# Layer 0 of a four-layer graph network: one excursion per tile, projections between weighing groups, the node bias hoisted, and the last norm in two parts

## The chip, the cores and the metric

The kernel runs on one core of a Trainium2 chip. The metric is the device time of one execution in microseconds. A core has five engines with queues of their own: TensorE (PE, with its weight loads counted apart as PEld), VectorE (DVE), ScalarE (ACT), GpSimd (POOL) and SyncE (SP, which here only issues transfers). Each engine takes its instructions in order. An instruction that waits holds up everything behind it on its engine, and nothing on the others, until one of them needs a result.

The kernel before takes 1303.24 us (median of 3 executions, 1303.01 to 1305.43).

## The reference

Four graph layers, each followed by a residual sum and a layer norm over the last axis. N is 2048 nodes, the batch B is 8, and there are C = 64 features. Only layer 0 and the first operations of layer 1 matter here.

```python
# layer 0, K = 3 polynomials of the adjacency matrix A, D = 16
w = einsum('nd,dkio->nkio', embedding, weight)      # weights per node
b = einsum('nd,do->no', embedding, bias)            # bias per node
As = [I, A, 2 A A - I]
x_g = einsum('knm,bmc->bnkc', stack(As), x)
out = einsum('bnki,nkio->bno', x_g, w) + b
x = layernorm(x + out)
# layer 1 begins with
h = x @ W
s = leaky_relu(h @ a_node, 0.2)                     # score of a node
alpha = softmax over nodes of s where H.T > 0
agg = einsum('ben,bnf->bef', alpha, h)
beta = sigmoid((h @ a_gn)[:, None, :] + (agg @ a_ge)[:, :, None])
industry = einsum('nm,bmf->bnf', adj / deg, x @ W_ind)
```

The later layers multiply by the adjacency matrix again and project; the change does not touch them.

## The kernel before

**Stages of layer 0.** Nodes go in 16 tiles of 128 (P = 128, NT = 16). The values of a tile, 8 batch elements of 64 features, are 512 columns (BC), and batch elements go in four pairs (NP), so that one transposed pair fills 128 partitions. `first_product` computes y1 = A x in 32 pieces of 16 matmuls, in four quarters of four tiles each, into accumulators of seven PSUM banks (`acc0`). The mask of non-zeros of A is multiplied, with x split in a high and a low part, and the row's scale is applied when the sum is read out (`y_hi` on ACT, `y_lo` on DVE). The weights `w0`, the embedding and the bias are loaded by `load_w0` (L235).

`layer0` (L1039) then goes through the tiles. For one tile j it holds:

- `weigh(j, g)`, L1172, for g = 0 to 7. Group g is half of the batch (4 elements) times 4 of the 16 embedding components. It makes 12 matmuls of 64 rows and 256 columns (the terms x, A x and A A x, for two pairs and two halves of the partitions), each recorded as two, into one of the two tiles of the pool `pps0` (two banks each), and then four `scalar_tensor_tensor` operations on DVE (L1193), which multiply by an embedding component and add into the residual `r`. The order in which they add is a chain on one buffer.
- `product(j)`, L1140: 32 matmuls of 512 columns that give A (A x) for the tile; ACT copies the result to `y` (L1151). `first_terms(j)`: transposes of A x and the node bias, one matmul of the transposed embedding `et` with `bias_sb` (L1126), and POOL's sum r0 = x + bias (L1131). `second_term(j)`: transposes of A A x.
- `scaled`, `compare`, `mask` and `degrees(j)`, L1080 to 1167: DVE makes the mask of the next tiles (L441), POOL scales it and sums it, DVE compares it with the matrix, and PE sums it to the degrees that later layers use. POOL's sum of both halves is called `both`.
- `normed(j, step)`, L1197: layer norm in three steps on DVE and ACT.
- For layer 1: `to_features(j)` (transposes of the normed x), `project(j)` (L1262 on, 16 matmul records, W and W_ind side by side in `wb`, into a `pps0` tile, read out by ACT and DVE), `scores(j)` (L1249, matmuls of 4 columns with `wa`), the weights exp(s), POOL's weighted features and their low part, and `gather(j)` (L1318), which adds to agg in a PSUM bank of its own.

**PSUM in layer 0.** The eight banks: one for layer 1's early product `fi`, one for agg (`fag`), two for transposes and small results (`trs0`, tag "tr"), and four for `pps0`.

**What sets the order.** `program_order()` (L212) fixes the written order on PE, DVE, ACT and POOL. The order of SP's transfers is left to the scheduler. The loop in L1389 to 1454 writes, after each group g of tile j, work for other tiles. Four times per tile there is work of 128 rows between groups of 64 rows: after g2 `first_terms(j+1)`, after g3 the projection, `product(j+1)` and `to_features(j-1)`, after g6 `second_term(j+1)`, `scores(j-1)` and `gather(j-2)`, after g7 `degrees(j+1)`:

```python
elif g == 3:
    when(j - 2, project)
    ...
        for _ in product(j + 1):
    ...
    when(j - 1, to_features)
...
elif g == 6:
    when(j + 1, second_term)
    when(j - 1, scores)
```

A last turn j = NT has no weighing; it is called the tail here. It holds the norm, transposes, scores and projection of tile 15, the denominators of the softmax (`denominators`, 32 small matmuls) and `industry_early`, the first of layer 1's products for the industry term: 16 steps of two matmuls of 512 columns, eight of them in the tail (five and three), seven in the beginning of layer 1 (four, one, two, at L598 to 620), and the last in the written sequence of layer 1's ramp, `early[0](NT)` at L1005. Buffers of layer 0 have homes in 16 slots of the retired split of x (`homes`, L1048).

## Time and profile before

| What | Value |
|---|---|
| Median of 3 executions | 1303.24 us |
| Profiled execution, its own time | 1302.44 us |
| Span of the profiled execution | 1300.7 us |
| Mean granted clock of TensorE | 0.976 |
| First product and its preparation | 0 to about 137 us |
| First weighing group of tile 0, of tile 1, of tile 2, of tile 15 | 156.71, 196.01, 228.03, 664.35 us |
| End of weighing | 691.14 us |
| DVE's first read of agg in layer 1 (L584) | 708.57 us |
| Three stretches of the span: PE busy | 126.80 of 131.00, 560.99 of 580.00 (131 to 711), 558.57 of 589.70 |

The profile is one execution, traced. The span goes from its first to its last instruction; the time has 1.74 us more around it. Busy times add up what an engine's instructions took. Matmuls are pipelined, and the ends of the records are modelled, so that prices of PE work are best read as differences between starts. "Waited for" names the engine whose result came last by the record. A page line gives busy us, share of the span and the number of instructions.

### The profile page before, as it was taken

What the parts mean: (1) busy time and instruction counts of PE and PEld (TensorE: products, weight loads), DVE (VectorE), ACT (ScalarE), POOL (GpSimd) and SP (SyncE); (2) the same over time, 40 slices, a digit from 0 to 9 for tenths busy, and PEclk for the clock granted to TensorE, in tenths of its full rate; (3) what the DMA queues carried; (4) which work ended last, traced back from release to release, by engine and by line L of the source; (5) the groups of instructions that cost most, each with busy time, mean ns of one, the idle gap of its engine ahead of it and who ended that gap; (6) DMA issues with size and microseconds to landing.
All of it is one profiled execution on the core that took longest, in us unless ns stands there. A gap on an engine that the chain in (4) does not pass through costs nothing. (4 is left out here: it accounts for less than half of the span.)

```text
span 1300.7 us, 20049 instructions
## 1 busy us (share of the span) xinstructions
PE 1246.4 (96%) x7724; PEld 1002.3 (77%) x7724; DVE 891.8 (69%) x1601; ACT 378.0 (29%) x853; POOL 512.1 (39%) x418
## 2 busy tenths in 40 slices
PE   9999789999999999999998799999998899999996
PEld 8787568888888888888886477777766788888885
DVE  4555268888887877888665777777774656565544
ACT  3000101221222222222222356666665521111111
POOL 1000354555554555555521578888871600000000
PEclk9999889999999999999999699999998999999998
DMA  8889533323333323222262322232220223334541
GB/s 283 249 236 174 179 97 102 107 99 106 108 108 108 108 100 97 95 97 105 81 234 66 113 76 98 102 102 99 84 83 1 97 98 130 121 106 154 194 170 67
DMA packets 100951, 157.22 MB, mean 121 GB/s; under 512 B 12912, under 2 KB 64496, under 8 KB 94832
## 3 DMA queue, kind: packets, MB, share of 16 engines
q1 hardware_dynamic: 98368, 151.65, 36.0%
q10 hardware_dynamic: 2304, 4.20, 0.8%
q8 instruction: 63, 1.03, 0.3%
q0 software_dynamic: 176, 0.02, 0.1%
q14 instruction: 40, 0.33, 0.1%
HBM read 118.08 MB, written 37.76 MB: 120 GB/s over the span
## 5 line engine op out<-in xcount | busy, mean ns | idle before, releaser
L1193 DVE SCALAR_TENSOR_TENSOR r<-pp,emb_sb,r 128x256 f32<-128x256 f32 x512 | 247.3, 483 | 110.2 <-PE pp L1182 95.4
L1182 PE MATMUL pp<-w_sb,xT 64*128 64x256 f32 x1024 | 161.5, 392 | 6.5 <-DVE r L1193 6.5
L1182 PE MATMUL pp<-w_sb,y2T 64*128 64x256 f32 x1024 | 154.6, 378 | 0.0
L1182 PE MATMUL pp<-w_sb,y1T 64*128 64x256 f32 x1024 | 154.6, 378 | 0.0
L1131 POOL TENSOR_TENSOR r<-xs,bn 128x256 f32<-128x256 f32 x32 | 22.7, 731 | 245.8 <-issue 217.2
L1182 PEld LDWEIGHTS pp<-w_sb,xT 64*128 64x128 f32 x1024 | 95.0, 187 | 24.7 <-issue 9.7
L1182 PEld LDWEIGHTS pp<-w_sb,y1T 64*128 64x128 f32 x1024 | 100.5, 188 | 11.0
L1182 PEld LDWEIGHTS pp<-w_sb,y2T 64*128 64x128 f32 x1024 | 100.4, 188 | 11.1
L524 PE MATMUL y1p<-x_hi,m 128*128 128x512 f32 x256 | 102.9, 402 | 1.0 <-DVE y_lo L539 1.0
L1145 PE MATMUL y2p<-y_hi,msk 128*128 128x512 f32 x256 | 103.5, 404 | 0.0
L1520 PE MATMUL ind<-y_hi,mj_l 128*128 128x512 f32 x240 | 101.8, 424 | 0.2 <-DVE dlt L843 0.2
L1145 PE MATMUL y2p<-y_lo,msk 128*128 128x512 f32 x256 | 101.4, 396 | 0.0
L524 PE MATMUL y1p<-x_lo,m 128*128 128x512 f32 x256 | 100.8, 394 | 0.2 <-DVE x_lo L464 0.2
L1520 PE MATMUL a<-v_hi,mj_l 128*128 128x512 f32 x256 | 100.1, 392 | 0.0
L1520 PE MATMUL a<-v_lo,mj_l 128*128 128x512 f32 x256 | 100.0, 391 | 0.0
L1520 PE MATMUL a<-y_lo,mj_l 128*128 128x512 f32 x240 | 95.1, 396 | 0.0
L1520 PE MATMUL a<-y_hi,mj_l 128*128 128x512 f32 x240 | 94.9, 395 | 0.0
L1520 PE MATMUL ind<-y_lo,mj_l 128*128 128x512 f32 x240 | 94.5, 394 | 0.0
L1084 POOL TENSOR_TENSOR ms<-msk,srow 128x1024 f32<-128x1024 f32 x32 | 90.2, 2819 | 10.0 <-DVE msk L441 5.1
L794 POOL TENSOR_TENSOR ez<-ez,coef 128x1024 f32<-128x1024 f32 x32 | 69.9, 2184 | 48.5 <-DVE ez L789 48.5
L441 DVE TENSOR_SCALAR msk<-adj 128x1024 fp32r<-128x1024 f32 x32 | 61.9, 1971 | 1.2 <-DMA adj<-in_at 1.2
L1145 PEld LDWEIGHTS y2p<-y_hi,msk 128*128 128x128 f32 x256 | 48.9, 191 | 13.0 <-issue 1.0
(294 smaller groups left out, 2434.1 us busy)
## 6 DMA issues: line engine op xcount, KB each, us to landing
mj_l<-mask SPq DMA_DIRECT2D x46, 1024.0 KB, 4.9
adj<-in_at SPq DMA_DIRECT2D x64, 256.0 KB, 3.9
mask<-msk SPq DMA_DIRECT2D x32, 512.0 KB, 4.6
raw<-in_at SPq DMA_DIRECT2D x31, 512.0 KB, 5.5
oh<-oh SPq DMA_DIRECT2D x32, 128.0 KB, 4.2
xT<-in_xt SPq DMA_DIRECT2D x16, 256.0 KB, 2.9
xs<-in_xn SPq DMA_DIRECT2D x16, 256.0 KB, 2.9
kept<-x SPq DMA_DIRECT2D x16, 256.0 KB, 2.0
```

What stands on the lines that cost most here:

```text
L441: nc.vector.tensor_scalar(r_(m), raw, 0.0, None, op0=ALU.is_gt)
L524: nc.tensor.matmul(accs[q][jj], r_(m[:, t, jj * P:(jj + 1) * P]), r_(part[:, mt, :]), start=i + h + t == 0 and part is x_hi, stop=i == 3 a ...
L794: nc.gpsimd.tensor_tensor(by_b(ezs[i]), by_b(ezs[i]), per_b(t["coef"], 2 * i, 2), ALU.mult)
L1084: nc.gpsimd.tensor_tensor(ms, m, srow[j].unsqueeze(1).to_broadcast([P, 8, P]), ALU.mult)
L1131: nc.gpsimd.tensor_tensor(r[:, 4 * bq * C:4 * (bq + 1) * C] .rearrange("p (h l c) -> p h l c", h=2, l=2), swapped(terms[j]["xs"], bq), bn. ...
L1145: nc.tensor.matmul(acc, r_(msk[j, mt // 8][:, mt % 8, :]), r_(part[:, mt, :]), start=mt == 0 and part is y_hi, stop=mt == NT - 1 and part ...
L1182: nc.tensor.matmul(pp[:, h, pl, :], terms[j][name][rs, 2 * bq + pl], w_sb[rs, k, dq * 4 * C:(dq + 1) * 4 * C], start=k == 0, stop=k == K - 1,)
L1193: nc.vector.scalar_tensor_tensor(rb, ppv[:, :, dd, :], emb_sb[:, j, d:d + 1], rb, op0=ALU.mult, op1=ALU.add)
L1520: nc.tensor.matmul(acc, r_(a[:, mt, :]), r_(part[:, mt, :]), start=mt == 0 and part is hi, stop=mt == NT - 1 and part is lo,)
```

## The change

**Node bias.** The bias of all 16 tiles is computed in the first product, at its second piece, into two of the accumulators, read out by ACT one piece later, and kept in `bn_all`. The transposed embedding comes by four transfers on ACT's queue into slots of `y_lo` that are not yet in use. The loads of `et` per tile, the bias matmul and its copy leave the loop.

**Weights.** `w0` and the embedding are fetched in seven pieces during pieces 10 to 16 of the first product, instead of by three transfers that are written after it.

**Excursion.** All work of 128 rows for a tile stands in one place, `visit(j)` after group 4. POOL's sum of the parts of A x (`first_sum`) is a function of its own, after g1, and r0 (`begin_sum`) is written after g5 of the tile before. `x` of a tile (`xs`) has one buffer instead of two, and is loaded after the tile before has read it.

**Projections.** `project` comes in two halves, after g5 and g7 (each with six copies on ACT and two subtractions on DVE), into the banks of the transposes. Two score columns stand beside W and W_ind in `wb` (130 columns), so that the scores come out of the projection; `scores` and `wa` are gone. The vectors for these columns are made after g5 of tile 0 (`score_weights`), not after its first group.

**Last tile.** Its norm, transposes, projections, weights and gathers come in halves of the batch (`half_normed`, `last_tile`), the first half's norm during g5 to g7. The tail holds two steps of `industry_early`; layer 1's ramp, which takes what is left, holds seven.

**Small.** Layer 1's constants `minus1` and `mhalf` are set on POOL instead of DVE. Buffers move between homes; the squares of the norm share the home of `y2`.

```diff
 def first_product(...):
+            def node_bias():
+                et, bn_all, rest = bias_in
+                b0 = bn_all[0:D, NT - 1, :]
+                for half in range(2):
+                    bp = ps_acc.tile([P, NT // 2, C], F32, tag="acc", name=f"bp_{half}")
+                    for t in range(NT // 2):
+                        j = half * (NT // 2) + t
+                        nc.tensor.matmul(
+                            bp[:, t, :], et[j // 4][0:D, (j % 4) * P:(j % 4 + 1) * P], b0,
+                            start=True, stop=True,
+                        )
...
+                    if n == 1:
+                        node_bias()
+                    elif n == 2:
+                        keep_bias()
+                    elif 10 <= n < 11 + 2 * K:
+                        midway(n - 10)
...
-        nc.vector.memset(minus1, -1.0)
+        nc.gpsimd.memset(minus1, -1.0)
...
-        def first_terms(j):
-            tr = ps_tr.tile([P, NP, P], F32, tag="tr", name=f"try1_{j}")
+        def first_sum(j):
             if j > 1:
-                y1 = tile("y1", f"y1_{j}", bufs=1)
-                nc.gpsimd.tensor_tensor(y1, y_hi[:, j, :], y_lo[:, j, :], ALU.add)
...
-            bp = ps_tr.tile([P, QW], F32, tag="tr", name=f"bp_{j}")
-            nc.tensor.matmul(bp[:, 0:C], terms[j]["et"], bias_sb, start=True, stop=True)
-            bn = tile("bn", f"bn_{j}", (P, C))
-            nc.scalar.copy(bn, bp[:, 0:C])
...
+        def half_normed(bq, step):
+            j = NT - 1
+            cols, bs = slice(4 * bq * C, 4 * (bq + 1) * C), slice(4 * bq, 4 * bq + 4)
...
+            elif step == 1:
+                nc.vector.tensor_reduce(var[:, bs], b_view(sq)[:, bs, :], AX.X, ALU.add)
+                nc.vector.tensor_scalar(var[:, bs], var[:, bs], EPS, None, op0=ALU.add)
+                nc.gpsimd.tensor_tensor(rstd[:, bs], var[:, bs], mhalf[:, bs], ALU.pow)
...
-        def scores(j):
...
+        def projected(j, n):
+            mms[j, n] = [
+                ps_tr.tile([P, 2, 2 * C + 2], F32, tag="tr", name=f"hp_{j}_{n}_{h}")
+                for h in range(2)
+            ]
+            for r in range(2):
                 for h in range(2):
...
+        def project(j, n):
+            projected(j, n)
+            for what in ("hi", "h", "sc", "lo"):
+                copied(j, n, what)
...
+        def weighted(j):
...
+            nc.gpsimd.tensor_tensor(r_(lo), hs, hi, ALU.subtract)
...
+        def visit(j):
+            when(j - 2, gather)
+            if j < NT - 1:
+                when(j - 1, normed, 2)
+            when(j + 1, compare, 0)
+            when(j + 1, first_terms)
+            if j + 1 < NT:
+                for _ in product(j + 1):
+                    pass
+            when(j + 2, mask, 0)
+            when(j + 2, mask, 1)
+            when(j + 1, compare, 1)
+            when(j - 1, to_features)
...
+            when(j + 1, second_term)
+            when(j + 1, degrees)
+
+        def last_tile():
+            trail = ("hi", "lo")
+            early.extend(industry_early())
+            half_features(0)
+            gather(NT - 2)
+            projected(NT - 1, 0)
+            half_normed(1, 0)
...
+            denominators(0, NT - 1)
+            half_normed(1, 1)
+            weights_of(NT - 1, slice(0, 4))
+            half_weighted(0)
+            half_gather(0)
...
+            half_normed(1, 2)
+            half_features(1)
+            projected(NT - 1, 1)
+            copied(NT - 1, 1, "sc")
+            weights_of(NT - 1, slice(4, 8))
+            half_weighted(1)
+            early[0](2)
+            denominators(NT - 1, NT)
+            half_gather(1)
...
                 for g in range(8):
-                    when(j, weigh, g)
+                    weigh(j, g)
...
                     elif g == 1:
+                        if j == 0:
+                            degrees(0)
+                        when(j + 1, scaled, 1)
+                        when(j + 1, first_sum)
+                    elif g == 2:
                         when(j - 1, normed, 1)
...
+                    elif g == 4:
+                        visit(j)
...
                     elif g == 5:
+                        if j == 0:
+                            score_weights()
+                        when(j + 2, scaled, 0)
+                        when(j + 1, begin_sum)
+                        when(j + 2, load_xs)
+                        when(j - 1, project, 0)
+                        if j == NT - 1:
+                            half_normed(0, 0)
+                            project(j - 1, 1)
+                            weights_of(j - 1)
...
+                    elif g == 7 and j < NT - 1:
+                        when(j - 1, project, 1)
+                        when(j - 1, weights_of)
+                        when(j - 1, weighted)
                     elif g == 7:
-                        when(j + 1, degrees)
-            early[0](3)
-            gather(NT - 1)
+                        half_normed(0, 2)
+            last_tile()
+            early.pop(0)
```

## The prediction

> **What bounds the kernel now.** I read the page first, for the engines:
>
> ```profile
> PE 1246.4 (96%) x7724; PEld 1002.3 (77%) x7724; DVE 891.8 (69%) x1601; ACT 378.0 (29%) x853; POOL 512.1 (39%) x418
> ```
>
> TensorE (PE) leads, but the change touches layer 0 alone, so I cut that layer into its stages with the view that gives busy time by stretch (start:end, length, then busy us of PE, its weight loads, DVE, ACT, POOL, and the granted clock):
>
> ```profile
> 131.00:156.70 25.70, 16.49 (x67) 12.73 (x65) 5.02 (x9) 3.92 (x7) 10.25 (x9) 0.80 0.64 211
> 156.70:196.00 39.30, 34.61 (x241) 27.99 (x240) 25.39 (x49) 1.55 (x4) 19.86 (x20) 0.91 0.29 89
> 228.00:664.30 436.30, 436.14 (x3448) 367.95 (x3448) 349.37 (x642) 98.03 (x196) 225.02 (x191) 1.00 0.33 111
> 664.30:691.10 26.80, 24.98 (x223) 22.13 (x223) 19.64 (x49) 6.60 (x13) 4.55 (x6) 1.00 0.30 82
> 691.10:708.60 17.50, 14.77 (x101) 12.21 (x100) 6.96 (x17) 4.35 (x10) 5.03 (x4) 0.90 0.10 31
> ```
>
> Tiles 2 to 14 (third row) leave PE 0.16 us idle in 436: there only fewer or shorter PE instructions help, and PE must stay fed. The handover from the first product, tile 0, tile 15 and the tail have holes. The waits of PE between 131 and 711 us name them (total, times, longest):
>
> ```profile
> PE pp L1182 <- DVE r L1193: 6.5, 4, 4.7
> PE bp L1126 <- DMA et<-in_embt: 6.3, 1, 6.3
> PE sgp L1249 <- ACT xT L1244: 2.2, 1, 2.2
> PE try L1118 <- DVE y_lo L539: 2.2, 1, 2.2
> ```
>
> The order of PE within one tile comes from its timeline (start, us, line):
>
> ```profile
> 336.52 0.66 PE L168 MATMUL try<-ident,y 128*128 128x128 f32 x4
> 337.11 0.43 PE L1126 MATMUL bp<-bias_sb,et 16*128 16x64 f32 x2
> 337.47 0.70 PE L1182 MATMUL pp<-w_sb,xT 64*128 64x256 f32 x4
> ...
> 340.16 1.06 PE L1270 MATMUL hp<-wb,xT 64*128 64x128 f32 x16
> 341.15 0.51 PE L1145 MATMUL y2p<-y_hi,msk 128*128 128x512 f32 x1
> ...
> 357.60 0.95 PE L1249 MATMUL sgp<-wa,xT 128*128 128x4 f32 x8
> 358.42 0.48 PE L1318 MATMUL aggp<-hs_hi,md 128*128 128x512 f32 x1
> 358.73 0.40 PE L1318 MATMUL aggp<-hs_lo,md 128*128 128x512 f32 x1
> 359.06 0.70 PE L1182 MATMUL pp<-w_sb,xT 64*128 64x256 f32 x4
> 361.85 0.27 PE L1167 MATMUL dgp<-ones_r,both 128*128 128x2 f32 x1
> ```
>
> Differences of starts are the prices: node bias .36, scores .82, gather .64, product 7.46 (341.15 to 348.61), a set of transposes .49 to .53, degrees .20, a weighing group 2.59. A tile is 33.48: eight groups 20.74, the rest 12.74.
>
> **What the Trainium skill says.** "TensorEngine Tiling (Array Packing)", Key Properties: changing the tiling mode drains TensorE. The trace agrees: four weighing matmuls next to a 128-row neighbour take .53 instead of .43 (337.47 to 338.00 against 338.00 to 338.44), .10 per switch. "TensorE: Matmul & The Clock Gate", its section on the clock gate: windows of 3413 ns, after an idle one half speed. The trace agrees: after the 6.3 us hole product(0) takes 9.53 against 7.46, and the 4.7 us hole is followed by 170.5 to 177.3 at half clock. "SBUF — State Buffer", Who interferes with whom: a DVE operation with two inputs in SBUF, or in a two-port mode, and GpSimd (POOL) lock each other out of a shared port. The trace agrees: POOL's `ms` takes 2.40 alone, up to 3.39 while DVE makes masks.
>
> **Part by part**, against the profiled execution (1302.44, span 1300.7); plus is gained.
>
> *Start.* Node bias: 16 products, 32 records, at .11 each (spacing of small matmuls in the trace; the skill's clock page, LDWEIGHTS section, gives about .107 for 128 columns): −3.5, between −2 and −4. It takes two of seven accumulator banks, so quarter 1 waits for three evictions instead of one: −1.2. Four more transfers on ACT's queue: −.3. Sum −5.0. The weights in six pieces: nothing. Their two loads already ran at 47.8 and 69.4, hidden under the product; without that cover 1.6 MB would cost several us.
>
> *Handover and tile 0.* The last first-product matmul starts at 135.3. Before, PE waited 2.2 for y_lo, 6.3 for et (queued on SP behind a transfer that waited for the last list store, landed 142.0), and ran product(0) at a reduced clock; weigh(0,0) at 156.71. After, the new bank order frees the transposes' bank about 1.4 earlier; no et, no bias matmul; product(0) 137.5 to 145.0; second transposes; weigh(0,0) 146.6: 10.1 sooner. But degrees(0), after g1, needs `both` from POOL and DVE: srow landed 144.93 and the chain from first `ms` to `both` took 10.44 (147.59 to 158.03), so 155.4. PE reaches it at 151.8: a new hole of 3.7, behind which g2 queues, and perhaps a half-clock window (0 to 1.7; I take 1.0). Gone is the 4.7 hole at 171 (DVE busy with the score weights, now after g5) with its slow windows. Tile 0 then sums to 146.6, eight groups 20.9 with their switch, the hole 3.7, the slow window 1.0, and an excursion of first transposes from both parts 1.04 (eight records at the .11 to .17 seen at 137.85), product 7.46, a wait of 1.0 for y2 (no other transposes to cover it), .5, .2, and two switches .2: weigh(1,0) at 182.6 instead of 196.0. +13.4, and +.3 in tile 1, whose gather is not yet there.
>
> *Tiles 2 to 14.* Removed: bias −.36, scores −.82, three of four pairs of mode switches −.60. Moved at equal cost: gather, product, transposes, degrees, first transposes, projections (2 × .45; two columns more). Added: a wait. second_term follows product and to_features directly; ACT's y2 copy takes .69 after the product's end, and the four transposes cover only part: .48 uncovered; .06 of widened projections. Net 1.78 − .54 = 1.24; period 32.24 (20.74 of groups, .9 of projections, 10.6 of excursion); ×13 = 16.1, and .4 for the tile with the flag: +16.5. Behind second_term on PE stand degrees and g5. Twelve ACT copies and four DVE subtractions more per tile are hidden: ACT was busy 98 of 436, DVE 349, so about 26.6 of 32.2 us a tile after.
>
> The cover that is thin is POOL: first_sum for j+1 is queued after scaled(j+1,1); From the tile's start: scores copied and exponentiated 2.7 (estimate: six ACT copies of .17 to .4, two small DVE operations, one more ACT), md .28, hs 1.04, ACT's high part .7, lo 1.26, `ms` 2.40, `cs` 1.27, .74 and .46, `both` .46, first sum 1.27: 12.6. PE needs it after five groups and gather, 12.95 + .1 + .64 = 13.7. The margin is 1.1 and no more; if it fails, first_terms waits, and product and all behind it.
>
> *Tile 15 and tail.* Tile 15 keeps one stall of about 2.0 (second half of project(14) waits for both transposes' banks) but loses its other extras: 25.3 against 26.8. Tail: from the last weighing to agg's first reader 17.43 now. After, the chain is: last scalar_tensor_tensor 2.2, the second half's norm and the first half's transposes meanwhile; gather(14) at 4.4 (its low part stands on POOL behind a pow, 1.68 for 8 columns); projections at 5.3; 30 denominators 3.37 to 8.7; half_gather(0) 9.2; half_features(1) 9.45; projected(15,1) 10.6; exp 11.7; half_weighted 12.25; half_gather(1) 12.8; copies, agg 13.25. So +1.5 + 4.2 − .5 for clock = +5.2. minus1 on POOL: agg's exp no longer waits behind DVE's flag work (709.26 to 709.92): +.6.
>
> *Ramp of layer 1.* Before, eight industry steps ran in tail holes; after, two. Twelve matmuls more at .23 to .43 in the ramp: −3.0 (0, if the ramp has holes that take them).
>
> Sum: −5.0 + 13.4 + .3 + 16.5 + 5.2 + .6 − 3.0 = 28.0, so 1274.4 for such an execution. The median shown, 1303.24, is .8 above the profiled one; I forecast 1275, and its own range is 1269 to 1281.
>
> **Rivals.**
> POOL late. If the shared port contends all along (the longest seen: `ms` 3.39, `cs` 1.74 and 1.06, first sum 2.25: 2.8 more), first_sum ends at 15.4, 1.7 us late per tile over 14 tiles: 24 of the gain gone, about 1299; half contended, .5 to 1 per tile, 1282 to 1289. For: such durations are in the trace; the excursion waits in one place for several releasers. Against: the typical durations are the lone ones, and DVE's masks, the worst contender, now come after the first sum.
> Switches become waits. PE saves no time in the loop since the y2 wait and the waits for transposes' banks take the 1.24 back; only the ends gain 11.5: about 1291. For: one excursion has no weighing between dependent steps. Against: the copies are short (.69) and banks are asked again only 2.6 us later.
> Better than that: y2's wait is covered and degrees(0) is not late (another 6 and 4.7): 1264 to 1267.
> Slower. POOL's queue before first_sum runs so late that PE waits over 2.0 us per tile: 14 × 2.0 eats the 28, at a chain 3.1 longer than the lone times; at 3 us a tile about 1317. For: `weighted` now adds md, hs and lo (.28 + 1.04 + 1.26) right before the next tile's chain. Against: POOL is busy 225 of 436, so lateness doesn't build up over tiles.
> The bias hoist doing nothing is no rival: its loop matmuls vanish from PE's order.
>
> **How the numbers follow.** Forecast case .55; better .12; POOL partly late .15; fully .06; switches become waits .07; slower .05. Below 1264 I leave 4 in 100; above 1290 about 14 (slower, fully late, a part of the rest). Range 1264 to 1290. A change of .2% (2.6 us) is about what a measurement here can tell: faster .93, same .02, slower .05.
>
> **What would show it.** Weigh-to-weigh period 32.2 with one long gap per tile between g4 and g5; PE waits: second_term on ACT's y copy about .5 per tile, degrees(0) on POOL's `both` about 3.7 once, none on the first sum; low clock at 140 to 150 and 170 to 177 gone; first product's end about 5 later; tail near 13. Wrong would be: first_terms waiting on POOL in every tile, a wait before the second projection half, DVE over 28 us per tile, or a first product longer by 8.

## The result, and the profile after

The changed kernel takes 1298.73 us (median of 20 executions, 1294.66 to 1303.17), the kernel before 1303.74 (20 executions, 1301.08 to 1307.74). The ratio is 0.9958, 95% interval 0.9947 to 0.9969: a gain of 0.4%, where 2.2% was forecast. The direction was right and the size was not: 1298.73 lies above the range.

The profiled execution of the changed kernel took 1296.06, with a span of 1294.3. Its page shows the engines as before:

```profile
PE 1228.0 (95%) x7598; PEld 1000.4 (77%) x7598; DVE 881.9 (68%) x1657; ACT 389.0 (30%) x987; POOL 503.4 (39%) x420
```

PE is busy 18.4 us less, but the span is only 6.4 shorter: 12 us of saved PE work came back as waiting. The starts of the first product's last piece and of the weighing groups, the end of weighing and agg's first read, side by side, show where:

| Stage | before | after | gain | forecast |
|---|---|---|---|---|
| Start of the last piece of the first product | 131.79 | 139.63 | −7.84 | −5.0 |
| from there to the first weighing group | 24.92 | 17.50 | +7.42 | +10.1 |
| tile 0 | 39.31 | 36.21 | +3.10 | +3.3 |
| tile 1 | 32.02 | 32.09 | −.07 | +.3 |
| tiles 2 to 14 | 436.32 | 426.99 | +9.33 | +16.5 |
| tile 15 | 26.87 | 27.95 | −1.08 | +1.5 |
| tail, to DVE's first read of agg | 17.36 | 19.61 | −2.25 | +3.7 |
| from there to the end | 592.13 | 594.31 | −2.18 | −2.4 |
| sum | 1300.7 | 1294.3 | +6.4 | +28.0 |

The table compares one execution of each kernel. Kernels of the experiments that leave a stage's code as the changed kernel has it show how far one such time can be trusted: the last piece starts at 138.8 to 142.0 (nine kernels), from there to the first weighing group it takes 15.9 to 19.1 (ten), tile 0 takes 34.65 to 38.68 (six), and tile 15 takes about 26.3 or 27.95 (seven, the changed kernel counted each time). The tail takes 19.61 or 19.62 in nine, and the usual period of a tile in the loop is 32.67 in seven. So the loop and the tail are read to a few hundredths, and the first stages only to about 2 us.

The view by stretch (start:end, length, busy us of PE, weight loads, DVE, ACT, POOL, then the granted clock) of the changed kernel:

```profile
11.00:23.00 12.00, 12.00 (x56) 10.02 (x55) 7.28 (x13) 4.47 (x9) 0.28 (x1) 0.72 0.94 336
143.00:157.13 14.13, 11.19 (x47) 8.47 (x45) 3.92 (x7) 2.87 (x5) 4.36 (x5) 0.88 0.82 278
157.13:193.35 36.22, 30.76 (x240) 25.92 (x239) 25.94 (x49) 1.59 (x4) 31.92 (x28) 1.00 0.36 109
225.44:652.43 426.99, 413.09 (x3322) 359.18 (x3320) 337.58 (x687) 106.07 (x300) 215.91 (x192) 1.00 0.34 113
652.43:680.40 27.97, 25.50 (x218) 22.40 (x214) 21.00 (x52) 9.60 (x30) 5.00 (x6) 0.94 0.31 83
680.40:700.00 19.60, 15.57 (x63) 12.84 (x64) 7.08 (x26) 4.35 (x20) 4.78 (x5) 0.57 0.08 27
```

Three rows matter. Around the bias block (first row) the clock is .72. In tiles 2 to 14 PE now has 13.9 us without work, where it had .16; DVE is busy 338 of 427 there, as foreseen. In the tail the clock is .57. The waits of PE between 139 and 690 us (total, times, longest) name the new ones:

```profile
PE pp L1221 <- DVE r L1232: 9.6, 16, 1.0
PE try L168 <- ACT y L1190: 7.2, 16, 0.8
PE dgp L1206 <- POOL both L1131: 3.0, 1, 3.0
PE trx_last L168 <- DVE x L1262: 2.8, 1, 2.8
PE try L1171 <- DVE y_lo L575: 2.2, 1, 2.2
PE hp L1336 <- DVE y_lo L1362: 1.9, 1, 1.9
```

The second and third were forecast at .5 per tile and 3.7. POOL's first sum is not among the waits, so that rival is out. The first is new: weighing waits for DVE in nearly every tile. DVE's timeline at the start of tile 5 shows what stands there:

```profile
328.00 2.04 DVE L1232 SCALAR_TENSOR_TENSOR r<-pp,emb_sb,r 128x256 f32<-128x256 f32 x4 [0.39 <-PE pp L1221]
329.96 0.68 DVE L1240 TENSOR_REDUCE s_l<-r 128x8 f32<-128x512 f32 x1
330.67 0.85 DVE L1241 SCALAR_TENSOR_TENSOR r<-s_l,r 128x512 f32<-128x512 f32 x1
331.45 4.18 DVE L1232 SCALAR_TENSOR_TENSOR r<-pp,emb_sb,r 128x256 f32<-128x256 f32 x8
335.54 0.68 DVE L1249 TENSOR_REDUCE var_l<-sq_l 128x8 f32<-128x512 f32 x1
```

The norm's first step, .68 and .85, delays the read-out of group 1, and PE's group 3, which needs its banks, comes late:

```profile
333.63 0.70 PE L1221 MATMUL pp<-w_sb,xT 64*128 64x256 f32 x4 [0.56 <-DVE r L1232]
```

The instructions stood behind the same group before, but `first_terms` was then between groups 2 and 3, and from group 2 to group 3 PE took 3.63 instead of 2.59: a microsecond for DVE. No run put `first_terms` back there; the experiments move and add DVE work instead.

### The profile page after: what moved, and what is told of

Same layout as the page of the kernel before. It is cut to its first block, busy times and chain, and to the rows that moved or that the text cites. A ratio compares the mean times of both kernels' runs of the same rounds, so it can differ in the third digit from the quotient of the medians.

```text
span 1294.3 us, 19958 instructions
## 1 busy us (share of the span) xinstructions
PE 1228.0 (95%) x7598; PEld 1000.4 (77%) x7598; DVE 881.9 (68%) x1657; ACT 389.0 (30%) x987; POOL 503.4 (39%) x420
## 3 DMA queue, kind: packets, MB, share of 16 engines
q8 instruction: 62, 1.02, 0.3%
## 4 chain that ended last, share of the span: by engine, by line
PE 76%; DVE 9%; issue 7%; ACT 2%; DMA 2%; POOL 2%; SPq 0%; DVEq 0%; ACTq 0%; POOLq 0%
PE a L1671 18%; PE pp L1221 18%; PE ind L1671 9%; PE y2p L1184 9%; PE y1p L560 5%; DVE r L1232 5%; PE fc L914 3%; PE df L923 2%; PE gp L795 1%; PE yp L1771 1%; PE try L168 1%; PE trm L168 1%; PE hp L1336 1%; PE red L844 1%; DVE r L1241 1%
## 5 line engine op out<-in xcount | busy, mean ns | idle before, releaser
L1120 POOL TENSOR_TENSOR ms<-msk,srow 128x1024 f32<-128x1024 f32 x32 | 87.0, 2720 | 103.0 <-DVE msk L449 93.3
L1221 PEld LDWEIGHTS pp<-w_sb,xT 64*128 64x128 f32 x1024 | 97.8, 188 | 25.2 <-PE pp L1221 15.6
L1221 PEld LDWEIGHTS pp<-w_sb,y1T 64*128 64x128 f32 x1024 | 104.1, 188 | 8.2
L1221 PEld LDWEIGHTS pp<-w_sb,y2T 64*128 64x128 f32 x1024 | 103.9, 188 | 8.3
L1136 DVE SCALAR_TENSOR_TENSOR ms<-ms,adj 128x1024 f32<-128x1024 f32 x32 | 71.0, 2224 | 0.0
L1403 POOL TENSOR_TENSOR hs<-h,es 128x512 f32<-128x512 f32 x15 | 15.6, 1042 | 129.2 <-ACT hgr L1375 129.2
L560 PEld LDWEIGHTS y1p<-x_hi,m 128*128 128x128 f32 x256 | 49.1, 192 | 12.2 <-ACT x_hi L471 0.9
```

The source lines that it names most:

```text
L560: nc.tensor.matmul(accs[q][jj], r_(m[:, t, jj * P:(jj + 1) * P]), r_(part[:, mt, :]), start=i + h + t == 0 and part is x_hi, stop=i == 3 a ...
L1120: nc.gpsimd.tensor_tensor(ms, m, srow[j].unsqueeze(1).to_broadcast([P, 8, P]), ALU.mult)
L1136: nc.vector.scalar_tensor_tensor(ms, ms, 1.0, raws[j][h], op0=ALU.mult, op1=ALU.not_equal, accum_out=bad[:, 2 * j + h:2 * j + h + 1],)
L1221: nc.tensor.matmul(pp[:, h, pl, :], terms[j][name][rs, 2 * bq + pl], w_sb[rs, k, dq * 4 * C:(dq + 1) * 4 * C], start=k == 0, stop=k == K - 1,)
L1403: nc.gpsimd.tensor_tensor(b_view(hs), b_view(h_sb[:, j, :]), bcast(es[:, j, :]), ALU.mult)
```

## Experiments

My theory was that the gain was lost in four separate places: (1) the bias block and the fetches in the first product, (2) DVE between weighing groups that now follow one another without a break, (3) in-order queues in tile 0, (4) a hole in the tail that brings the half clock. The common rival: PE's switches and the transposes' two banks cost as much as they save, or POOL is late. All edits are against the changed kernel. Ratios are to the kernel before on the same chip. A kernel for which no ratio is given was executed once, so that only its trace counts.

### The loop: parting the norm, moving it, adding to it

First the norm was spread over the groups, with the same work:

```diff
                     if g == 0:
...
-                        when(j - 1, normed, 0)
+                        when(j - 1, normed, -1)
                     elif g == 1:
+                        when(j - 1, normed, 0)
...
-                    elif g == 2:
+                    elif g == 3:
                         when(j - 1, normed, 1)
```

Step −1 is the sum, step 0 now the subtraction alone, step 1 the variance.

> Edit: the layer norm's first step in the loop is parted: the sum stays behind group 0, the subtraction goes behind group 1, the variance from behind group 2 to behind group 3. Same work. In the changed kernel PE waits .56 in every tile before group 3 (for r on DVE), period 32.67. Theory (DVE has two PSUM buffers of slack, some .5 us per group, and 1.5 us of norm in one place is more than that): the wait before group 3 falls under .1, period 32.0 to 32.2, tiles 2 to 14 in 417 to 421 instead of 427, time about .6% less than the changed kernel. Rival (DVE is slowed by the port it shares with POOL, or PE by its own switches): the wait moves to another group and the period stays at 32.5 to 32.7.

1293.07 (ratio 0.9918, 0.9894 to 0.9941). The wait before group 3 is gone (2.59), but group 4 now starts 3.05 after group 3, not 2.66: period 32.39. The subtraction, behind group 1, took 1.34 (median over the tiles) where the changed kernel had .85: POOL was scaling a mask beside it, and it reads two operands in SBUF. Neither side was right in full: the place matters, but behind group 1 the lengthened operation still costs PE .46.

So the subtraction, variance and scaling went into the excursion, where DVE idled 2.2 us before the first group behind it:

```diff
             when(j - 2, gather)
             if j < NT - 1:
+                when(j - 1, normed, 0)
+            when(j + 1, compare, 0)
+            if j < NT - 1:
+                when(j - 1, normed, 1)
+            when(j + 1, compare, 1)
+            if j < NT - 1:
                 when(j - 1, normed, 2)
-            when(j + 1, compare, 0)
             when(j + 1, first_terms)
...
             when(j + 2, mask, 1)
-            when(j + 1, compare, 1)
```

> Edit: of the layer norm in the loop only the sum stays behind group 0; the subtraction, the variance and the scaling stand in the excursion, between and after the two compares, and the masks behind them. Same work as the changed kernel; tile 14 keeps its old places. Parting the norm between groups only moved half of the wait (period 32.39 instead of 32.67, with .46 before group 4): the subtraction took 1.34 instead of .85 there. Theory (between groups DVE has some .5 us of slack per group and POOL lengthens what reads two SBUF inputs; in the excursion DVE has room): groups 0 to 4 follow one another at 2.59 to 2.66, the excursion stays at 10.1 to 10.3, period 32.0 to 32.2, tiles 2 to 14 in 417 to 421. Rival (DVE's work in the excursion is full as well): x comes late for to_features or y2T for group 5, the excursion is above 10.6 and the period 32.4 or more.

1283.33, ratio 0.984 (0.9813 to 0.9868). Groups 0 to 4 follow at 2.59 each, the excursion takes 10.12, the period is 31.84, tiles 2 to 14 take 415.16 instead of 426.99, a little better than the theory's 417. The subtraction takes .68. Of the 9.6 us that PE waited for r, .4 is left; the y2 wait stands as it was (waits of PE, 0 to 720 us):

```profile
PE try L168 <- ACT y L1190: 7.2, 16, 0.8
...
PE dgp L1206 <- POOL both L1131: 3.6, 1, 3.6
...
PE pp L1221 <- DVE r L1232: 0.4, 1, 0.4
```

The edit does a second thing that I had not planned. Both compares now stand ahead of the masks, in a stretch where POOL is idle, and the 32 compares take 1.22 in the median instead of 1.59. With the same instructions DVE is busy 846.0 us over the span instead of 881.9, and POOL 481.7 instead of 503.4. So this run alone does not part the place of the norm from a DVE that is less disturbed.

The next one does. How much room there is was measured by giving DVE more of the same sum, in six tiles of that kernel (the sums are read by nothing):

```diff
+        doses = {(8, 0): 1, (9, 0): 2, (10, 0): 3, (11, 0): 4, (12, 2): 3, (13, 1): 2}
...
                     weigh(j, g)
+                    if (j, g) in doses:
+                        for n in range(doses[j, g]):
+                            spare = tile("var", f"spare_{j}_{n}", (P, B), 1)
+                            nc.vector.tensor_reduce(spare, b_view(resid[j]), AX.X, ALU.add)
```

> On the kernel with the norm in the excursion (period 31.84, only one sum of .68 behind group 0): further sums of the same .68, whose results nothing reads, are put on DVE: 1, 2, 3 and 4 behind group 0 of tiles 8 to 11, 3 behind group 2 of tile 12, 2 behind group 1 of tile 13. Theory (between groups DVE has .55 idle and the two banks forgive about .45 more; PE meets a late read-out two groups on; behind group 2 it meets it only after the excursion, so it is free): stalls before group 3 of .4, 1.1, 1.7 and 2.4 in tiles 8 to 11, periods 32.2, 32.9, 33.6, 34.2; tile 12 stays at 31.8 to 31.9 with 2.0 us more on DVE; tile 13 waits about .45 before group 4. Rival (DVE has room on the average, 20 per cent idle, and catches up; the wait before group 3 had another cause, such as POOL): tiles 8 and 9 within .1 of 31.84. Rival (any work on DVE costs PE its whole length): tile 8 32.5, tile 12 33.9.

PE's timeline, the first matmuls of group 3 in tiles 8 to 11 and of group 4 in tile 13:

```profile
425.71 0.70 PE L1221 MATMUL pp<-w_sb,xT 64*128 64x256 f32 x4 [0.46 <-DVE r L1232]
458.98 0.70 PE L1221 MATMUL pp<-w_sb,xT 64*128 64x256 f32 x4 [1.18 <-DVE r L1232]
492.98 0.70 PE L1221 MATMUL pp<-w_sb,xT 64*128 64x256 f32 x4 [1.90 <-DVE r L1232]
527.69 0.70 PE L1221 MATMUL pp<-w_sb,xT 64*128 64x256 f32 x4 [2.62 <-DVE r L1232]
594.96 0.70 PE L1221 MATMUL pp<-w_sb,xT 64*128 64x256 f32 x4 [0.74 <-DVE r L1232]
```

The first further sum costs .63 on PE and each one after it .72, its whole length, as the second rival says for this place: the periods are 32.55, 33.27, 33.99, 34.74 (the idle by modelled ends is .17 less than the starts give). In tile 13, with two sums behind group 1, group 4 starts .90 late, where I had .45. From group 2 to group 3 PE takes 3.22, 3.94, 4.66 and 5.38 instead of 2.59. The line through these four points meets 2.59 at about .1 of a sum, so the room behind group 0 is the first sum, .7 us, and hardly more; my 1.0 was too large. Three sums behind group 2 cost nothing (tile 12: 31.83), as what they delay is group 5, and the excursion comes first; here that rival is out by 2 us. That settles the cause in the loop: not the average load of DVE, but what stands between it and the second group after it.

Then the y2 wait, by work that could cover it:

```diff
-            when(j + 1, first_terms)
             if j + 1 < NT:
                 for _ in product(j + 1):
...
+            when(j + 1, first_terms)
+            when(j + 1, degrees)
             when(j + 1, second_term)
-            when(j + 1, degrees)
```

> Edit: in the excursion first_terms and degrees stand between to_features and second_term, instead of ahead of the product and behind second_term; the same work. In the changed kernel PE waits .40 per tile, 7.2 in all, for ACT's copy of y2. Theory (the wait is uncovered time of that copy, .73 more of PE work covers it): the excursion falls by .3 to .4, from 10.15, unless ACT's copy of the first transposes holds the bank; period 32.3. Rival (ACT's three copies in a row are the limit: y, xT, y1T, .69 + .58 + .59, two banks): the wait goes on, for ACT's xT, and the period stays within .1 of 32.67.

The rival's mechanism held, and the cost was more than it allowed: period 33.10, .43 worse. PE waits twice, for the banks of the transposes:

```profile
PE dgp L1206 <- ACT xT L1314: 6.1, 14, 0.4
PE try L168 <- ACT deg L1209: 3.6, 15, 0.6
```

### The start

```diff
                     if n == 1:
-                        node_bias()
+                        spread.append(node_bias())
...
-                    elif 10 <= n < 11 + 2 * K:
-                        midway(n - 10)
+                    elif 20 <= n < 21 + 2 * K:
+                        midway(n - 20)
...
+                            if n in (1, 2):
+                                next(spread[0], None)
```

(`spread` is a generator that yields after one tile's bias; the last line stands behind the matmuls of one of four accumulators, x high and low.)

> Edit: the 16 node-bias matmuls are spread, one after every second large matmul of pieces 1 and 2 of the first product, and the seven fetches of weights and embedding move from pieces 10 to 16 to pieces 20 to 26. In the changed kernel the first product's last piece starts at 139.63, before the change at 131.79, 7.84 apart: 4.4 for the bias block, 2.1 for piece 1 at a lower clock (granted 0.72 in 11 to 23 us), 1.9 for a raw block that came late before piece 17, less 1.3 for a wait for a bank that is gone. Theory (clock and collision): a solid block of small matmuls lets the clock fall, and the fetches collide with the matrix's blocks. Then the clock in 11 to 23 is above 0.95, the pause before piece 17 is under 0.4, and the last piece starts at 134 to 136. Rival (raw price): the records cost .14 each wherever they stand, and the pause has another cause: last piece at 138.5 to 140.

The pause before piece 17 is gone (piece 16: 3.77 instead of 5.68). In the changed kernel DVE, which makes the mask for that piece, waits for a block of the matrix:

```profile
79.82 0.69 DVE L519 TENSOR_SCALAR m<-raw 128x1024 fp32r<-128x1024 f32 x1 [2.16 <-DMA raw<-in_at]
```

Moving the fetches removes the pause, here and in all later kernels that move them, so they cause it; how they delay the block is not shown. But the last piece started at 140.76. Pieces 1 and 2 took 8.67 and 8.19, at a granted clock of 1.00. Neither theory had this. The timeline of PE shows the price:

```profile
13.20 0.43 PE L484 MATMUL bp<-bn_all,et 16*128 16x64 f32 x2
13.55 0.51 PE L564 MATMUL y1p<-x_hi,m 128*128 128x512 f32 x1
13.90 0.39 PE L564 MATMUL y1p<-x_lo,m 128*128 128x512 f32 x1
14.22 0.43 PE L484 MATMUL bp<-bn_all,et 16*128 16x64 f32 x2
```

From bias to bias 1.02, for two large matmuls that take .46 alone: .56 for one tile's bias, where in a block it takes .28 at the lower clock. So the changes between the two kinds of matmul cost about as much again as the matmuls. Hence two blocks, ahead of pieces 3 and 5, with the fetches left at pieces 20 to 26:

```diff
-                    if n == 1:
-                        node_bias()
+                    if n in (3, 5):
+                        node_bias((3, 5).index(n))
```

> Edit: the node bias in two blocks of eight tiles, ahead of pieces 3 and 5 of the first product, and the fetches of weights at pieces 20 to 26. Spread singly it cost 10.0 over pieces 0 to 2, at a full clock, with .34 and .68 from one matmul to the next; as one block ahead of piece 1 it cost 7.1, at a granted clock of .72. Theory (each change between 16-row and 128-row matmuls costs about .1 both ways, and a block longer than a clock window lets the clock fall): two short blocks pay few changes and keep the clock; they cost 3.4 to 4.2 in all, pieces 1 and 4 after them take 3.7 to 3.9 and the last piece starts at 134.5 to 136. Rival (small 16-row matmuls cost more than their spacing, however they stand): the last piece starts at 138 or later.

The last piece starts at 134.71, against 138.8 to 142.0 with the single block and the early fetches. The blocks take 1.9 each, .12 per record, and the clock holds:

```profile
11.00:23.00 12.00, 12.00 (x60) 9.75 (x59) 7.46 (x13) 3.76 (x7) 1.20 (x2) 1.00 0.96 336
```

So the single block costs 4.4 itself and 2 to 3 us by the clock after it; the fetches cost 1.9. A single block ahead of a later piece was not tried, so its length and its early place are not parted.

### Handover and tile 0

```diff
                     elif g == 1:
-                        if j == 0:
-                            degrees(0)
...
                     elif g == 4:
+                        if j == 0:
+                            degrees(0)
                         visit(j)
+                        if j == 0:
+                            score_weights()
...
                     elif g == 5:
-                        if j == 0:
-                            score_weights()
```

> Edit: degrees of tile 0 behind group 4 instead of group 1, and the score vectors on DVE right behind the first excursion's work instead of behind group 5. In the changed kernel tile 0 takes 36.21: PE waits 3.0 for POOL's sum before degrees(0), and 1.65 before tile 1's first group. Theory: POOL's sum is late only because PE asks for it early, and the second wait is DVE's delay by eight small operations: tile 0 takes 31.5 to 32.5. Rival (POOL's whole chain is late): PE waits in the excursion instead, for the masks or the sums of tile 1, and tile 0 stays above 34.

Tile 0 took 35.49. That is on the rival's side, but the unedited tile 0 takes 34.65 to 38.68, so the size says little; the waits say more. PE no longer waits for POOL; it waits for r before groups 3 and 7, 1.5 and 2.7 longer than 2.59. DVE has both compares behind group 0, and its eight operations for the score vectors took 5.1 instead of 2.7, one of them 2.06 instead of .28, beside POOL's work. So the order on DVE went next (the two compares of tile 0 behind groups 1 and 2, the score vectors in the excursion ahead of `to_features`), with degrees(0) behind group 4 and the product of tile 0 ahead of its first transposes:

```diff
             begin_sum(0)
             load_xs(1)
-            first_terms(0)
             scaled(0, 0)
             scaled(0, 1)
             for _ in product(0):
                 pass
+            first_terms(0)
...
                     elif g == 1:
-                        if j == 0:
-                            degrees(0)
+                        if j == 0:
+                            compare(0, 0)
...
+                    elif g == 2 and j == 0:
+                        compare(0, 1)
```

> Edit, handover and tile 0 alone: the product of tile 0 stands ahead of its first transposes; degrees(0) behind group 4; the two compares of tile 0 behind groups 1 and 2 instead of both behind group 0; the score vectors on DVE in the first excursion ahead of to_features' place. In the changed kernel: 2.16 idle for the last y_lo, the product at a reduced clock (9.1 busy), 3.0 before degrees(0), 1.65 before tile 1; first weighing group 17.5 after the last piece starts, tile 0 36.2. With degrees and score vectors moved alone, tile 0 took 35.5, as the wait became one for r behind DVE's compares and behind score vectors that took 5.1 instead of 2.7. Theory (DVE's in-order queue is what PE meets in tile 0, and the last y_lo is needed only by the product's end): no idle before the product, weighing 13.5 to 14.5 after the last piece's start; tile 0 at 33 to 34.5. Rival (POOL's chain from srow is late in itself): with weighing earlier the compares wait for POOL by as much, and tile 0 stays above 36.

Tile 0 took 33.71, and from the last piece to weighing it took 15.03, instead of 17.50. Together that is 48.7; the kernels with both stages unedited take 52.4 to 54.6. The idle before the product did not go:

```profile
145.56 0.50 PE L1184 MATMUL y2p<-y_hi,msk 128*128 128x512 f32 x1 [2.16 <-DVE y_lo L575]
```

The product writes another bank than the transposes, and its first matmul reads tile 0's parts, ready long before; it still starts when the last y_lo of the first product is done. So the wait is not that of one bank, as I had it. What it is (all banks of the retired pool at once, for instance) stays open; it was not tried. The gain came from y2's copy, which the transposes now cover (.78), and from the product, 7.6 busy instead of 9.1; the latter is not to be counted on, since it is the clock's: full here, and with all edits together half for 3.4 us, with the product at 9.2 again. Tile 0 is within what was expected.

### Tile 15 and the tail

```diff
             early.extend(industry_early())
+            denp.append(ps_p.tile([P, 2, 2, 4 * C], F32, tag="pp", name="denp")[:, 0, 0, 0:B])
+            denominators(0, NT - 1)
             half_features(0)
...
-            denominators(0, NT - 1)
             half_normed(1, 1)
```

> Edit: in the last tile's tail the first 30 denominators (with their buffer) stand first, ahead of the first half's transposes. In the changed kernel PE idles 2.83 us at 680.4 (for x from DVE), the granted clock in 680.4 to 700 is .57, the 30 denominators take 6.4 instead of 3.4, and the tail is 19.6 instead of 17.4. Theory (the hole lets the clock fall, and that makes the tail long): the denominators fill the hole, take 3.4, the clock is above .8, and agg is read 3 to 5 us earlier after the last weighing (14.5 to 16.5). Rival (the tail is a chain over DVE, ACT and POOL that the place of the denominators doesn't touch): the holes move behind them, and the tail stays at 18.5 or more.

1290.88, ratio 0.9904 (0.9882 to 0.9926). The tail is 14.46, but what follows takes 596.1 instead of 594.3, so that 3.4 of the 5.2 are left. The 30 denominators, in the kernel before, in the changed kernel, and then here:

```profile
691.14 3.52 PE L1335 MATMUL denp<-es,md 128*128 128x8 f32 x30
```

```profile
683.22 0.57 PE L168 MATMUL trx_last<-ident,x 128*128 128x128 f32 x2 [2.83 <-DVE x L1262]
...
686.93 6.57 PE L1431 MATMUL denp<-es,md 128*128 128x8 f32 x30
```

```profile
683.71 3.52 PE L1431 MATMUL denp<-es,md 128*128 128x8 f32 x30
687.08 0.65 PE L168 MATMUL trx_last<-ident,x 128*128 128x128 f32 x2
```

Before the change they stood first in the tail, right behind the weighing; the change had moved them behind the hole, and this edit puts them back. The denominators alone, by stretch (the granted clock is the third number from the end), in the changed kernel and then here:

```profile
686.93:693.35 6.42, 6.42 (x33) 6.42 (x31) 1.64 (x7) 1.34 (x8) 0.00 (x0) 0.50 0.11 42
```

```profile
683.71:687.08 3.37, 3.37 (x31) 3.37 (x31) 3.21 (x8) 0.62 (x1) 2.47 (x4) 1.00 0.30 78
```

The clock over the tail is .65 all the same, not the .8 I asked for: it falls to .5 at 687, right behind the 30 small matmuls, which themselves ran at 1.00. The filled hole (2.83) and the denominators at full clock (3.05), less a new hole of 1.58 before the first half_gather, make 4.3 of the 5.2. With four and four steps of `industry_early` in those holes, and the second half of tile 14's projection behind group 6 instead of group 5:

```diff
-                            project(j - 1, 1)
-                            weights_of(j - 1)
                     elif g == 6:
                         if j == NT - 1:
+                            projected(j - 1, 1)
...
+                            weights_of(j - 1)
+                            weighted(j - 1)
                             half_normed(0, 1)
-                            weighted(j - 1)
...
             half_weighted(0)
+            gather(NT - 2)
+            early[0](4)
             half_gather(0)
...
-            early[0](2)
+            early[0](4)
```

> Only tile 15 and the tail of the changed kernel edited: denominators first with four and four early industry steps in the holes behind, the second half of tile 14's projection behind group 6, gather of tile 14 later. With the denominators alone first, the tail took 14.46 instead of 19.6, and the beginning of layer 1 lost 1.8 of that again. Theory: tile 15 24 to 25.5 instead of 27.97, tail 13.5 to 15, and twelve matmuls fewer in the ramp win 1 to 2; together 8 to 11 less than the changed kernel, median 1287 to 1291. Rival (the tail's end is the chain norm, transposes, projection, weights on DVE and ACT, and steps in its holes delay it): tail 16 or more, median above 1293.

1284.41, ratio 0.9862 (0.9845 to 0.9879). Tile 15 takes 23.9. The tail is 16.15, on the rival's side, but what follows takes 592.6, about as before the change (592.1). Against the denominators alone the steps cost 1.7 in the tail and 3.4 come back behind it. With these large matmuls in the holes the clock over the tail is .79. The sum of the three is what counts: 632.7 against 641.9 in the changed kernel and 638.5 with the denominators alone. The median lies below the theory's range and far below the rival's.

### All together

What held was put in one kernel: two blocks and later fetches, tile 0's order, the norm in the excursion, the tail with denominators first and eight steps, minus1 on DVE.

> Edits that held, together: bias in two blocks and later fetches; product of tile 0 first, degrees(0), compares and score vectors of tile 0 moved; norm in the excursion; denominators first in the tail with eight early industry steps in the holes behind them; minus1 and mhalf set on DVE again. Theory (the causes are apart, so the gains add): against the changed kernel's profile (span 1294.3) start 4.9, handover and tile 0 4.9, tiles 2 to 14 11.8, tail 5.1 and ramp 1.7 from the steps: span about 1266, median 1268 to 1273, ratio to before .973 to .977. Rival (they meet: a stall gone in one place opens the next one behind it, as in tile 0): 1276 or more.

1266.56, ratio 0.9718 (0.9699 to 0.9737), slightly better than the theory's range. The gains add: start 3.8, handover and tile 0 4.2, tiles 2 to 14 11.7, tail 4.3 and what follows 1.9, each within 1.1 of what was expected, and 3.2 more in tiles 1 and 15. With the four parts of the score vectors made one at a time behind groups 5, 6, 7 and the next group 0, and tile 15's order from above:

```diff
                     elif g == 5:
+                        if j == 0:
+                            score_weights(0, 0)
...
                     elif g == 6:
+                        if j == 0:
+                            score_weights(0, 1)
```

> As the one with all edits, and two more: the four parts of the score vectors stand singly behind groups 5, 6 and 7 of tile 0 and group 0 of tile 1; in tile 15 the second half of the projection of tile 14 comes behind group 6 instead of behind group 5, its low parts behind group 7, and the gather of tile 14 behind the first half's weights. In the changed kernel tile 15 took 27.97, with 5.8 from group 5 to group 6 (two groups' banks for the transposes not read out yet). Theory (a DVE insertion of .5 to .7 fits between groups, and the banks are free one group later): tile 0 loses the 1.8 before group 7, tile 15 takes 24 to 25.5, together 3 to 4.5 less than with all edits: 1264 to 1270. Rival (the small operations are lengthened by POOL to 1 or 2 us each; tile 15's end is DVE's chain): within 1.5 of the one with all edits.

1262.49, ratio 0.969 (0.9674 to 0.9706): faster than both kernels, by 3.1% against the one before. Tile 0 takes 31.49 instead of 32.85, and tile 1 31.88 instead of 31.36, since the part behind its group 0 delays group 3. Tile 15 takes 23.1.

## Why the prediction was wrong, point by point

**Tiles 2 to 14 (7.2 of the 21.6 that are missing).** The step "hidden: DVE 26.6 of 32.2 us a tile" failed. The average was about right (338 of 427, which is 26.0 a tile), the conclusion not: I had removed the work of PE that stood between groups 2 and 3, and did not ask what it gave DVE time for. The wait before group 3 and its trace cost .8 per tile (3.32 and 2.66 from group to group instead of 2.59 twice), DVE's late read-outs in tiles 2 and 4 another 1.7 (33.14 and 33.87 against 32.67); the other terms gave .4 per tile back. The rest of the sum stood: y2's wait .40 against .48, the excursion 10.15 against 10.6, the two projection halves 1.0 against .9. With the norm in the excursion the loop gains 21.2, more than I forecast. POOL's margin held.

**Start (2.8).** The records were .138 each, not .11 (.12 in the short blocks), and the clock stood at half from 14.33, within the block, to 21.15, five microseconds behind its end. I had the Trainium skill's "TensorE: Matmul & The Clock Gate", its section on the clock gate, in hand and thought of idle windows only. PE was busy by the record all along. "The weights in six pieces: nothing" failed too: at pieces 10 to 16 they held up a block of the matrix for 1.9. Against this the 1.2 for the banks did not come; a wait of 1.3 at piece 8 went instead.

**Handover (2.7).** "The new bank order frees the transposes' bank" failed: 2.16 is 2.16. Why the wait stays is open, as said above. With it stayed a part of the slow clock (product 9.1 busy, .88); in three kernels with the same code there the clock stayed full, and the stage took 15.9 instead of 17.5. The removal of et and bias, 6.3, held.

**Tile 0 (.2).** Right in size, by luck. The wait for `both` was 3.0 of 3.7, and the score vectors still cost 1.65 behind group 5; the slow window did not come. These errors cancel in this execution. In the one with the denominators first, where tile 0 is the same code, PE waited 3.7, the half clock came from 168.3 to 171.7, and tile 0 took 38.68.

**Tile 15 and tail (2.6 and 5.9).** The projection's bank wait came as forecast, 1.9 for 2.0; what I had at nothing is the stretch at half clock behind it, 673.1 to 676.5. In two kernels with the same code it did not come, and tile 15 took 26.3 instead of 27.95: that is 1.7 of the 2.6, and the rest stays open. In the tail I let the norm of the first half be done when PE wants it. It was 2.83 late, the denominators stood behind the hole instead of in it, and ran at half clock: 6.4 against 3.4. Both are terms of that sum; putting them first, where the kernel before had them, takes back 5.2.

**minus1 (.6).** Nothing came of it. The memsets on POOL waited for DVE's flag, as the timeline of POOL shows:

```profile
701.49 0.10 POOL L602 MEMSET minus<- 128x1 f32 x1 [15.22 <-DVE flag L1733]
```

agg is read at 699.99, and ACT's exp starts 1.63 later; before, 1.35, and with the memsets on DVE again in the kernel with all edits 1.34.

**Ramp.** The time from agg on lost 2.2, where −2.4 was forecast. That fits only roughly: −2.4 has the .6 for minus1 in it, which did not come, and putting the 12 matmuls back into the tail returned 1.7 against the changed kernel, of 3.0 allowed.

Rivals: "POOL late" in full names the measured time (about 1299), but by chance, since no wait is for POOL's sum. "Switches become waits" is nearest in kind, but the new waits in the loop were for DVE's read-outs, not for the banks of the transposes. Five stages (start, handover, loop, tile 15 and tail) erred the same way. In two of them work had been taken away from beside what it covered: PE's transposes beside DVE's norm, and the denominators that had filled the beginning of the tail.

## What to carry to other kernels

When work between two groups is taken away, ask which engine used that time: here PE's transposes between groups 2 and 3 gave DVE a microsecond, and without them .7 us per tile is what the two PSUM buffers forgive behind group 0. A share of 80% says nothing of that; count what DVE does from one group to the next but one. Here small matmuls were cheapest in short blocks, neither singly nor in one long row. Fill the first hole of a tail with the work that needs nothing from it.

## What the runs showed of the hardware that I had not expected

- Small matmuls kept the clock low although PE was busy by the record: a block of 32 records of 16 rows and 64 columns, 4.4 us long, ended and was followed at half speed; two blocks of 16, 1.9 us each, kept the full clock. In the tail 6.42 us of 8-column matmuls without a gap stayed at .50 from end to end, and in the four kernels with the 30 denominators put first the clock fell right behind them. In the kernel before it did not: there ten matmuls of 512 columns follow at once. The Trainium skill, "TensorE: Matmul & The Clock Gate", its section on the clock gate, has the clock rise after some 3.4 us sustained; in these runs such matmuls did not raise or hold it by themselves.
- A DVE operation with two SBUF inputs beside POOL was stretched by up to 2.2 us, where POOL's scaling takes 2.40 alone: a compare from 1.22 to 3.43, the subtraction from .68 to 1.34 in the median of one kernel, a 64-column product from .25 to 2.06. The Trainium skill, "SBUF — State Buffer", Who interferes with whom, says that this happens; the sizes are of these traces.
- A change from 128-row to 16-row matmuls and back cost about .3 in all (.56 singly against .24 in a short block).
